# Fillings of the expert table one tile ahead, and earlier reads of the last sums, in a hybrid convolution, scan and mixture-of-experts kernel

## The chip, the cores and the metric

The kernel runs on one core of a Trainium2 chip, as a single program. The metric is the device time of one execution in microseconds (us). The engines are named as the profile names them: PE is the matrix engine and PEld its weight loads, DVE the vector engine, ACT the scalar engine, POOL is GpSimd, and SP issues most of the DMA transfers. "L2029" is line 2029 of the kernel before, unless the line is said to be of the kernel after.

## The reference

The input is x of shape (2, 256, 48, 48), float32. Two layers follow each other. Layer 0 adds to x a convolution branch and a local attention branch over 7 by 7 neighbourhoods. Layer 1 turns the picture into 2 x 2304 = 4608 tokens of 256 channels, adds a gated state-space scan, and then a mixture of 8 experts of which every token takes its best 2. The last part is what the change touches:

```python
xf = x.reshape(-1, D)                       # 4608 tokens, D = 256
gate_logits = xf @ Wg + bg                  # 8 experts
top_w, top_i = jax.lax.top_k(gate_logits, 2)
top_w = jax.nn.softmax(top_w, axis=-1)
w_dense = jnp.sum(jax.nn.one_hot(top_i, E) * top_w[..., None], axis=1)
out = jnp.zeros_like(xf)
for e in range(E):
    h = jax.nn.gelu(xf @ W1[e] + b1[e], approximate=False)   # 256 -> 1024
    out = out + w_dense[:, e:e + 1] * (h @ W2[e] + b2[e])    # 1024 -> 256
...
t = t + out.reshape(B, L, D)                # and t goes back to (2, 256, 48, 48)
```

The kernel computes only the two experts that each token takes: it sorts the tokens by expert and runs every expert over its own tokens.

## The kernel before

**The table of tokens.** While the scan of layer 1 is finished chunk by chunk, each chunk of 128 tokens is normalized, its two experts are found, and its rows (256 channels, 8 gate values and the token's number: 1060 bytes) are written by POOL's indirect transfers (L1679) into a table `xs` in DRAM. Each expert has its own part of the table, `PART` rows long, and the rows come in order of arrival. `taken` holds, for every expert, the last row that it has used.

**Tiles.** The expert stage works through the table in tiles. A pair is 256 rows of one expert, a single is 128 rows. The list `tiles` has 33 pairs with 4 singles among them. Which expert and which rows a tile has is known only when all tokens have been counted; `plan()` and `plan_tiles()` work it out on DVE from the counts, with a dozen small comparisons and sums over 33 x 8 and 8 x 8 numbers. The plan's answer is `where`, one small integer table for the pairs and one for the singles: row 0 has the first row of a tile in `xs` (L1963), row 1 the place of the expert's weights (L1964). SP loads such a number into a register when it issues a transfer. Three tiles of expert 0 have been computed earlier, beside the end of the scan (the lines up to L1843); the plan is issued behind the second to last of these (L1833 is their last step on DVE).

**Fillings.** An expert's last tile mostly runs over the end of its rows. So behind the last row of each expert a filling is written: rows of zeros (`none`) whose token numbers point to spare rows of the result. In the kernel before, `fill(e)` does that for all eight experts at the border between the scan and the expert loop (L2006, called in a loop behind the plan): 256 rows for expert 0, 128 rows for the others. Its start is `ends`, the rows of `taken` plus one, which needs no plan. The group "fill" of `declare_no_dep` tells the scheduler that a filling and the other accesses of the table in that group need not wait for each other; the group "rows" says the same for fillings and scatters.

**The loop.** For tile i, `fetch(i)` brings its rows from `xs` into `ex` (L2029, three buffers), and `load(i)` brings the biases `bt` (L2019) and the weights `wt` (L2021, 2 MB, three buffers). `turn(i)` transposes the rows on PE (L902), copies them (L904), and works out on DVE each row's gate weight (`own` L2041, `weight` L2045) and its token number (L2047). `up(i)` multiplies by the first weights (L2085) with the gelu on ACT (L2089). `weight_sums` and `hidden_sums` (L2059 to L2062, L2071 to L2074) are additions on DVE for a scheme that gets a pair's second product with 7 block products in place of 8; `down(i)` does these (L2128) and combines them (L2132 to L2141), a single goes by L2113. `finish` scales by the gate weight (L2094) and adds the rows into a table `acc` in DRAM by an indirect transfer (L2095). At the end of tile i, `fetch(i + 3)` and `load(i + 3)` are issued. All transfers of SP are kept in the order of the program; `load(i + 3)` waits for a weight buffer, that is for the last matmul of tile i.

**The end.** `results()` reads the sums from `acc` in 12 blocks of 384 tokens. The first 8 blocks are read before the last tiles are done, the last 4 ("late reads", L2201) afterwards. It goes through the blocks two by two: PE transposes them (L2226), DVE and ACT copy them (L2229), and for each pair of blocks one store goes out on SP and one on ACT (L2232). In the kernel before, the late reads are issued when the pass reaches block 8, so SP has issued its stores of blocks 0, 2, 4 and 6 ahead of them.

The scheduler orders each engine's instructions by a model of their costs; where `keep_in_program_order` is called, the order of the program holds.

Of the kernel before, what the change touches and what calls it, by code (L numbers as in the profile page):

```python
# [32 lines left out]
I32 = mybir.dt.int32  # L33
AF = mybir.ActivationFunctionType
ALU = mybir.AluOpType
AX = mybir.AxisListType

P = 128
# [27 lines left out]
TB = NJ * P  # L66
# [4 lines left out]
E, HID = 8, 1024  # L71
NHC = HID // P

TR = 256
CAP = B * N
PART = CAP + TR
EARLY, NEARLY = 3, 3
NPAIR, NSINGLE = 2 * B * N // TR - NEARLY, E
# [40 lines left out]
def bcast(ap, axis, shape):  # L119
    return ap.unsqueeze(axis).to_broadcast(shape)  # L120
# [108 lines left out]
class Kernel:  # L229
# [1625 lines left out]
    def plan(self):  # L1855

        nc, begun = self.nc, [5 * TR] * NH

        def new(*shape, dtype=F32):
            size = int(np.prod(shape))  # L1860
            h = next(h for h in range(NH) if begun[h] + size <= N)
            t = self.x[1][:, h, begun[h] : begun[h] + size]
            begun[h] += size
            if len(shape) > 1:
                names = "abc"[: len(shape)]
                t = t.rearrange(f"p ({' '.join(names)}) -> p {' '.join(names)}", **dict(zip(names[1:], shape[1:])))
            return t.bitcast(dtype) if dtype != F32 else t

        vec = nc.vector
        scratch = new(NPAIR * 2 * E)  # L1870

        def piece(*shape):
            t = scratch[:, : int(np.prod(shape))]
            names = "abc"[: len(shape)]
            return t.rearrange(f"p ({' '.join(names)}) -> p {' '.join(names)}", **dict(zip(names[1:], shape[1:])))

        last_rows = new(E, dtype=I32)
        vec.tensor_scalar(last_rows, self.taken, 1.0, None, ALU.add)
        return last_rows, partial(self.plan_tiles, new, piece)

    def plan_tiles(self, new, piece):

        nc, vec, n, k, tid = self.nc, self.nc.vector, P, CAP // TR, self.c["tid"]
        tri = self.c["tri"].rearrange("p (a b) -> p a b", a=E)
# [63 lines left out]
        for which, row, behind in ((pwhich, prow, late), (swhich, srow, None)):  # L1948
            count = which.shape[-1]
            shape = [n, count, E]  # L1950
            to, hot, past = new(2, count, dtype=I32), new(count, E), new(count)
            vec.scalar_tensor_tensor(row, which, float(PART), row, ALU.mult, ALU.add)
            vec.tensor_tensor(hot, bcast(which, 2, shape), bcast(tid[:, :E], 1, shape), ALU.is_equal)
            if behind is not None:
                own = piece(count, E)
                vec.tensor_tensor(own, hot, bcast(first, 1, shape), ALU.mult)
                vec.tensor_reduce(past, own, AX.X, ALU.add)
                vec.tensor_tensor(past, past, behind, ALU.mult)
                vec.scalar_tensor_tensor(row, past, float(TR), row, ALU.mult, ALU.add)
            vec.tensor_tensor(hot, hot, bcast(self.ahead, 1, shape), ALU.mult)  # L1960
            vec.tensor_reduce(past, hot, AX.X, ALU.add)
            vec.tensor_add(row, row, past)
            vec.tensor_scalar(to[:, 0, :], row, float(E * PART), None, ALU.min)  # L1963
            vec.tensor_scalar(to[:, 1, :], which, float(E - 1), float(P), ALU.min, ALU.mult)  # L1964
            where.append(to)
# [16 lines left out]
    def experts(self, ctx):  # L1982
# [16 lines left out]
        nfirst, load_sums = BEFORE // NJ, self.load_sums  # L1999
        tiles += [(1, i) for i in range(NUSUAL, NSINGLE)]  # L2000

        def fill(e):
            row = self.value(ends[0:1, e : e + 1], sp, NROWS - TR)
            rows = P if e else TR
            put = self.tc.keep_in_program_order(
                nc.sync.dma_start(self.expert_rows(self.xs[bass.ds(row, rows), :]), self.none[:, : rows // P])  # L2006
            )
            self.tc.declare_no_dep(put.ins, group="fill", reason="every part of the table has its own")
            self.tc.declare_no_dep(put.ins, group="rows", reason="the rows of an expert end before")
            self.tc.add_to_no_dep_group("fill", put.ins)  # L2010

        def load(i):
            halves, n = tiles[i]
# [128 lines left out]
                    finish(i, y, j)  # L2142
            del weights[i], turned[i], hidden[i]

        ends, plan_tiles = self.plan()
        with self.tc.issue_after(self.adds[NEARLY - 2].ins):
            where, many = plan_tiles()
        for e in range(E):
            fill(e)
        load(0)  # L2150
        fetch(0)
        fetch(1)
        load(1)
        load(2)
        fetch(2)
        with self.tc.issue_after(self.adds[NEARLY - 1].ins):
            turn(0)
            weight_sums(0)

        def run(first, end):  # L2160
            for i in range(first, end):
                up(i)
                if i + 1 < end:
                    turn(i + 1)
                if i in sums:
                    hidden_sums(i)
                down(i)
                if i + 1 < end:
                    weight_sums(i + 1)
                if i + 3 < end:  # L2170
                    fetch(i + 3)
                    load(i + 3)
                if i + 4 == usual:
                    for g in range(nfirst):
                        load_sums(g, "first sums")
# [2 lines left out]

        with self.tc.If(self.value(many[0:1, 0:1], list(self.nc.engines), NSINGLE) > NUSUAL):
            for i in range(usual, usual + 3):  # L2180
                fetch(i)
                load(i)
            turn(usual)
            run(usual, len(tiles))
            for g in range(nfirst):
                load_sums(g)
# [21 lines left out]
    def results(self, pool):  # L2208

        nc = self.nc  # L2210

        first, size, n = BEFORE // NJ, 2 * TB, 0
        for g in range(0, B * NBLK, 2):
            b, blk = divmod(g, NBLK)
            if g == first:
                for i in range(first, B * NBLK):
                    self.tc.keep_in_program_order(self.load_sums(i))
            for k in range(NH):
                if n % (WMAT // size) == 0:
                    space = pool.tile([P, WMAT], F32, tag="wt", name="o")  # L2220
                o = space[:, n % (WMAT // size) * size :][:, :size].rearrange("p (i t) -> p i t", i=2)
                n += 1
                for i in range(2):
                    ps = self.bank()
                    for j in range(NJ):
                        nc.tensor.transpose(  # L2226
                            ps[:, j * P : (j + 1) * P], self.sums_block(g + i)[:, j, k * P : (k + 1) * P], self.ident
                        )
                    (nc.vector.tensor_copy, nc.scalar.copy)[i](  # L2229
                        o[:, i].rearrange("c (p j) -> c j p", j=NJ), ps[:, :TB].rearrange("c (j p) -> c j p", j=NJ)  # L2230
                    )
                (nc.sync, nc.scalar)[k].dma_start(self.out[b, k * P : (k + 1) * P, blk * TB : (blk + 2) * TB], o)  # L2232

    def run(self):
        nc = self.nc
# [130 lines left out]
```

## Time and profile before

| | us |
|---|---|
| median of 3 runs | 1292.45 (1290.72 to 1294.8) |
| the profiled execution | 1295.8 |
| its span | 1294.0 |
| PE busy in the span | 1232.5 (95%), mean granted clock 0.986 |
| DVE, ACT, POOL busy | 924.8, 792.7, 557.6 |
| start of the fillings (L2006) | 753.86 |
| first fetch (L2029) | 780.83 |
| first matmul of the expert loop (L2085) | 790.70 |
| last matmul of the expert loop (L2113) | 1268.9 |
| first early store, first late read, last store issued | 1272.23, 1277.93, 1290.34 |

Times in the profile count from the start of the span. A timeline's line has the start, the length, the engine, the line, the operation, output and input; "x8" means that many instructions were put together; in brackets stands how long the engine was idle before it and what ended the wait. "issue" is a wait for nothing that the profile shows. SPq and ACTq are the queues of SP and ACT, that is the issue of their transfers, not the transfers themselves.

### The profile page before, as it was taken

What the parts mean: (1) busy time and instruction counts of PE and PEld (TensorE: products, weight loads), DVE (VectorE), ACT (ScalarE), POOL (GpSimd) and SP (SyncE); (2) the same over time, 40 slices, a digit from 0 to 9 for tenths busy, and PEclk for the clock granted to TensorE, in tenths of its full rate; (3) what the DMA queues carried; (4) which work ended last, traced back from release to release, by engine and by line L of the source; (5) the groups of instructions that cost most, each with busy time, mean ns of one, the idle gap of its engine ahead of it and who ended that gap; (6) DMA issues with size and microseconds to landing.
All of it is one profiled execution on the core that took longest, in us unless ns stands there. A gap on an engine that the chain in (4) does not pass through costs nothing. (4 is left out here: it accounts for less than half of the span.)

```text
span 1294.0 us, 23558 instructions
## 1 busy us (share of the span) xinstructions
PE 1232.5 (95%) x8048; PEld 983.4 (76%) x8048; DVE 924.8 (71%) x2425; ACT 792.7 (61%) x1954; POOL 557.6 (43%) x769
## 2 busy tenths in 40 slices
PE   4999999998799999999999997999999999999995
PEld 3566766665567777777777786999999999999994
DVE  5899999999577887879797745555654665566442
ACT  2598978898799888789697552333333333333342
POOL 4411230210357878999889963212121212221220
PEclk9999999999799999999999998999999999999998
DMA  7331322211132234333636238657667667666756
GB/s 283 126 104 41 100 92 76 80 49 41 43 107 89 91 116 120 116 114 120 187 117 186 64 133 278 184 169 254 203 221 236 192 198 228 235 188 199 233 178 208
DMA packets 101658, 194.12 MB, mean 150 GB/s; under 512 B 10635, under 2 KB 82652, under 8 KB 96604
## 3 DMA queue, kind: packets, MB, share of 16 engines
q1 hardware_dynamic: 85020, 168.51, 38.3%
q0 software_dynamic: 14400, 19.74, 7.8%
q10 hardware_dynamic: 2116, 4.33, 1.0%
q8 instruction: 66, 1.08, 0.3%
q14 instruction: 56, 0.46, 0.1%
HBM read 154.24 MB, written 43.23 MB: 153 GB/s over the span
## 5 line engine op out<-in xcount | busy, mean ns | idle before, releaser
L2095 POOL DMA_INDIRECT acc<-ey,token x70 | 108.7, 1552 | 368.5 <-ACT ey L2094 312.1
L2085 PE MATMUL bank<-ext,wt 128*128 128x256 f32 (+1 forms) x1152 | 241.3, 368 | 0.0
L2089 ACT ACTIVATE hid<-bank,bt 128x256 f32<-128x256 f32 (+1 forms) x288 | 132.3, 461 | 170.7 <-PE bank L2085 166.5
L2085 PEld LDWEIGHTS bank<-ext,wt 128*128 128x128 f32 x1152 | 207.0, 190 | 25.0
L681 POOL COPY kp<-kp 128x10 f32<-128x10 f32 (+1 forms) x60 | 24.9, 415 | 179.4 <-DVE kp L674 179.4
L592 DVE SCALAR_TENSOR_TENSOR x<-hid,w2r,x 128x1128 f32<-128x1128 f32 (+3 forms) x72 | 99.9, 1392 | 0.4 <-ACT hid L586 0.2
L2128 PE MATMUL po<-ts,ss 128*128 128x128 f32 x768 | 96.2, 275 | 0.0
L916 PE MATMUL bank<-xn,win 128*128 128x387 f32 x240 | 92.7, 510 | 2.1 <-ACT t L999 2.1
L1129 DVE SCALAR_TENSOR_TENSOR xc<-bank,vec,xc 128x384 f32<-128x384 f32 x144 | 86.6, 610 | 8.4 <-ACT xc L1118 8.1
L2128 PEld LDWEIGHTS po<-ts,ss 128*128 128x128 f32 x768 | 90.9, 192 | 0.0
L1345 ACT ACTIVATE mt<-mt,cum 128x128 f32<-128x128 f32 x288 | 87.8, 393 | 1.7 <-DMA mt<-decays 1.7
L800 ACT ACTIVATE prob<-prob,top 128x308 f32<-128x308 f32 x144 | 78.3, 552 | 16.0 <-DVE top L789 15.6
L1679 POOL DMA_INDIRECT xs<-u,rows x72 | 72.9, 1012 | 17.4 <-issue 14.7
L2132 ACT COPY u<-po 128x128 f32<-128x128 f32 x32 | 8.5, 266 | 114.2 <-PE po L2128 114.2
L2072 DVE TENSOR_TENSOR ss<-hid 128x512 f32<-128x512 f32 x32 | 22.1, 691 | 70.6 <-ACT hid L2089 70.6
L1451 PE MATMUL bank<-wout,y 128*128 128x264 f32 x288 | 72.0, 396 | 0.1
L916 PE MATMUL zbank<-xn,win 128*128 128x384 f32 x192 | 71.2, 492 | 0.5 <-ACT z L1247 0.3
L806 ACT ACTIVATE prob<-prob,rden 128x308 f32<-128x308 f32 x144 | 67.7, 550 | 3.7 <-DVE rden L855 3.7
L582 DVE SCALAR_TENSOR_TENSOR hid<-xp,vec,hid 128x1175 f32<-128x1175 f32 (+1 forms) x48 | 68.4, 1425 | 0.1
L2128 PE MATMUL po<-wt,hid 128*128 128x128 f32 x496 | 65.5, 275 | 0.0
L789 DVE CUSTOM_DVE_ANT_0 prob<-banks,cst 128x308 f32<-128x308 f32 x144 | 61.7, 471 | 3.9 <-PE banks L779 3.6
L916 PEld LDWEIGHTS bank<-xn,win 128*128 128x128 f32 x240 | 42.5, 195 | 24.8 <-issue 3.9
(334 smaller groups left out, 2989.6 us busy)
## 6 DMA issues: line engine op xcount, KB each, us to landing
wt<-in_We SPq DMA_DIRECT2D x36, 2048.0 KB
mt<-decays SPq DMA_DIRECT2D x36, 512.0 KB
ex<-xs SPq DMA_DIRECT2D x36, 265.0 KB
rd<-decays SPq DMA_DIRECT2D x68, 128.0 KB
val<-vtab SPq DMA_DIRECT2D x72, 110.0 KB
bt<-in_We SPq DMA_DIRECT2D x36, 136.0 KB
vraster<-vout SPq DMA_DIRECT2D x18, 256.0 KB
acc<-x SPq DMA_DIRECT2D x36, 128.0 KB
```

The lines of the kernel that those rows point to most:

```text
L582: nc.vector.scalar_tensor_tensor(dst, src, w[:, k : k + 1], dst, ALU.mult, ALU.add)
L592: nc.vector.scalar_tensor_tensor(dst, src, w[:, k : k + 1], dst, ALU.mult, ALU.add)
L800: nc.scalar.activation(t, t, AF.Exp, bias=T["top", c][:, a : a + 1], scale=-1.0, accum_out=T["den", c][:, a : a + 1])
L916: self.nc.tensor.matmul(ps, lhsT=lhs(k), rhs=rhs(k), start=k == 0, stop=k == NH - 1)
L1129: nc.vector.scalar_tensor_tensor(out(), T["bank", ("cv", at)][:, i : i + TB], wc[:, i : i + 1], out(), ALU.mult, ALU.add)
L1345: nc.scalar.activation(t, t, AF.Relu, bias=at_s, scale=-1.0)
L1451: nc.tensor.matmul(ps[:, : C + E], lhsT=T["y", c][:, m, :], rhs=self.l1["wout"][:, m, :], start=m == 0, stop=m == NZ - 1,)
L1679: ins = nc.gpsimd.indirect_dma_start(self.xs, bass.IndirectOffsetOnAxis(ap=of("rows")[:, i, q : q + 1], axis=0), T["u2", g][:, i, :], None,)
L2085: nc.tensor.matmul(ps[:, :rows], lhsT=w1[:, k, c * P : (c + 1) * P], rhs=xt[:, k, :], start=k == 0, stop=k == NH - 1,)
L2089: nc.scalar.activation(hid[:, c, :], ps[:, :rows], AF.Gelu, bias=bt[:, c : c + 1])
L2095: put = nc.gpsimd.indirect_dma_start(self.acc, bass.IndirectOffsetOnAxis(ap=token[:, j : j + 1], axis=0), y, None, compute_op=ALU.add)
L2128: nc.tensor.matmul(p[name], lhsT=v[a][:, c], rhs=v[w][:, c], start=c == 0, stop=c == NHC // 2 - 1)
```

## The change

The fillings are now made per tile. `where` gets a third row: for each tile, the end of its expert's rows, worked out in `plan_tiles()` by a product and a sum over the experts, with a place behind the whole table for tiles that have no expert. `fill(i)` writes 128 rows there, and is called one tile ahead of the fetch that may need them: `fill(0)` (256 rows, by `first_end`, which needs no plan) and `fill(1)` ahead of the loop, then `fill(i + 4)` behind `load(i + 3)`. The group "fill" is gone, so that the scheduler orders fillings and fetches of the table: a fetch waits until the filling before it has landed, and a filling until the fetch before it has landed. `fill(i)` is called for every tile, so an expert's filling is written again for each of its tiles. In `results()` the late reads are issued when the pass reaches block 4 in place of block 8, that is behind SP's second store; and the stores are kept in the order of the program.

```diff
@@ -1869,16 +1869,17 @@
         vec = nc.vector
         scratch = new(NPAIR * 2 * E)
 
-        def piece(*shape):
-            t = scratch[:, : int(np.prod(shape))]
+        def piece(*shape, at=0):
+            t = scratch[:, at : at + int(np.prod(shape))]
             names = "abc"[: len(shape)]
             return t.rearrange(f"p ({' '.join(names)}) -> p {' '.join(names)}", **dict(zip(names[1:], shape[1:])))
 
-        last_rows = new(E, dtype=I32)
+        last_rows, first_end = new(E), new(1, dtype=I32)
         vec.tensor_scalar(last_rows, self.taken, 1.0, None, ALU.add)
-        return last_rows, partial(self.plan_tiles, new, piece)
-
-    def plan_tiles(self, new, piece):
+        vec.tensor_copy(first_end, last_rows[:, 0:1])
+        return first_end, partial(self.plan_tiles, new, piece, last_rows)
+
+    def plan_tiles(self, new, piece, last_rows):
 
         nc, vec, n, k, tid = self.nc, self.nc.vector, P, CAP // TR, self.c["tid"]
         tri = self.c["tri"].rearrange("p (a b) -> p a b", a=E)
@@ -1948,9 +1949,15 @@
         for which, row, behind in ((pwhich, prow, late), (swhich, srow, None)):
             count = which.shape[-1]
             shape = [n, count, E]
-            to, hot, past = new(2, count, dtype=I32), new(count, E), new(count)
+            to, hot, past, end = new(3, count, dtype=I32), piece(count, E, at=NPAIR * E), new(count), new(count)
             vec.scalar_tensor_tensor(row, which, float(PART), row, ALU.mult, ALU.add)
             vec.tensor_tensor(hot, bcast(which, 2, shape), bcast(tid[:, :E], 1, shape), ALU.is_equal)
+            own = piece(count, E)
+            vec.tensor_tensor(own, hot, bcast(last_rows, 1, shape), ALU.mult)
+            vec.tensor_reduce(end, own, AX.X, ALU.add)
+            vec.tensor_scalar(past, which, float(E), float(E * PART), ALU.is_ge, ALU.mult)
+            vec.tensor_tensor(end, end, past, ALU.max)
+            vec.tensor_copy(to[:, 2, :], end)
             if behind is not None:
                 own = piece(count, E)
                 vec.tensor_tensor(own, hot, bcast(first, 1, shape), ALU.mult)
@@ -1999,15 +2006,17 @@
         nfirst, load_sums = BEFORE // NJ, self.load_sums
         tiles += [(1, i) for i in range(NUSUAL, NSINGLE)]
 
-        def fill(e):
-            row = self.value(ends[0:1, e : e + 1], sp, NROWS - TR)
-            rows = P if e else TR
+        def fill(i):
+            if i >= len(tiles):
+                return
+            halves, n = tiles[i]
+            at = where[2 - halves][0:1, 2, n : n + 1] if i else first_end[0:1]
+            row = self.value(at, sp, NROWS - TR)
+            rows = P if i else TR
             put = self.tc.keep_in_program_order(
                 nc.sync.dma_start(self.expert_rows(self.xs[bass.ds(row, rows), :]), self.none[:, : rows // P])
             )
-            self.tc.declare_no_dep(put.ins, group="fill", reason="every part of the table has its own")
             self.tc.declare_no_dep(put.ins, group="rows", reason="the rows of an expert end before")
-            self.tc.add_to_no_dep_group("fill", put.ins)
 
         def load(i):
             halves, n = tiles[i]
@@ -2142,17 +2151,19 @@
                     finish(i, y, j)
             del weights[i], turned[i], hidden[i]
 
-        ends, plan_tiles = self.plan()
+        first_end, plan_tiles = self.plan()
         with self.tc.issue_after(self.adds[NEARLY - 2].ins):
             where, many = plan_tiles()
-        for e in range(E):
-            fill(e)
+        fill(0)
         load(0)
         fetch(0)
+        fill(1)
         fetch(1)
         load(1)
         load(2)
+        fill(2)
         fetch(2)
+        fill(3)
         with self.tc.issue_after(self.adds[NEARLY - 1].ins):
             turn(0)
             weight_sums(0)
@@ -2170,6 +2181,8 @@
                 if i + 3 < end:
                     fetch(i + 3)
                     load(i + 3)
+                    if i + 4 < end:
+                        fill(i + 4)
                 if i + 4 == usual:
                     for g in range(nfirst):
                         load_sums(g, "first sums")
@@ -2178,8 +2191,10 @@
 
         with self.tc.If(self.value(many[0:1, 0:1], list(self.nc.engines), NSINGLE) > NUSUAL):
             for i in range(usual, usual + 3):
+                fill(i)
                 fetch(i)
                 load(i)
+            fill(usual + 3)
             turn(usual)
             run(usual, len(tiles))
             for g in range(nfirst):
@@ -2212,7 +2227,7 @@
         first, size, n = BEFORE // NJ, 2 * TB, 0
         for g in range(0, B * NBLK, 2):
             b, blk = divmod(g, NBLK)
-            if g == first:
+            if g == first // 2:
                 for i in range(first, B * NBLK):
                     self.tc.keep_in_program_order(self.load_sums(i))
             for k in range(NH):
@@ -2229,7 +2244,9 @@
                     (nc.vector.tensor_copy, nc.scalar.copy)[i](
                         o[:, i].rearrange("c (p j) -> c j p", j=NJ), ps[:, :TB].rearrange("c (j p) -> c j p", j=NJ)
                     )
-                (nc.sync, nc.scalar)[k].dma_start(self.out[b, k * P : (k + 1) * P, blk * TB : (blk + 2) * TB], o)
+                self.tc.keep_in_program_order((nc.sync, nc.scalar)[k].dma_start(
+                    self.out[b, k * P : (k + 1) * P, blk * TB : (blk + 2) * TB], o
+                ))
 
     def run(self):
         nc = self.nc
```

## The prediction

> **What bounds the kernel now.** I read the busy shares, then stretches of 50 us, then the queue, matmul, vector and GpSimd timelines around the two places the diff touches: the border before the expert loop (753 to 800 us) and the end (1270 us on).
>
> ```profile
> span 1294.0 us, 23558 instructions
> PE 1232.5 (95%) x8048; PEld 983.4 (76%) x8048; DVE 924.8 (71%) x2425; ACT 792.7 (61%) x1954; POOL 557.6 (43%) x769
> ```
> ```profile
> 900.00:950.00 50.00, 50.00 (x349) 47.03 (x348) 30.86 (x80) 15.88 (x37) 10.98 (x7) 1.00 0.61 189
> 950.00:1000.00 50.00, 50.00 (x337) 46.71 (x336) 27.60 (x74) 19.19 (x47) 12.39 (x8) 1.00 0.72 230
> ```
>
> The second fence has stretch, length, then busy time of PE, PEld, DVE, ACT and POOL, the granted clock, the DMA share and GB/s. From 800 to 1250 us PE is busy 50.00 of every 50.00 us: the loop is bound by matmuls, and what the change adds there costs nothing unless it makes PE wait. So time can come or go only at the border and at the end.
>
> The border, as queue, matmul, vector and GpSimd timelines (start, length, engine, line):
>
> ```profile
> 753.86 8.32 SPq L2006 DMA_DIRECT2D xs<-none  x8
> 780.83 4.00 SPq L2029 DMA_DIRECT2D ex<-xs  x2
> 785.88 0.34 SPq L2021 DMA_DIRECT2D wt<-in_We  x1
> 788.08 3.24 SPq L2029 DMA_DIRECT2D ex<-xs  x2
> ```
> ```profile
> 775.09 1.89 PE L1805 MATMUL bank<-x,wt 128*128 128x256 f32 x8
> 783.62 5.70 PE L1821 MATMUL bank<-wt,x 128*128 128x256 f32 x16 [6.64 <-issue]
> 789.15 0.60 PE L902 MATMUL bank<-cst,ex 128*128 128x128 f32 x4
> ```
> ```profile
> 783.74 0.26 DVE L1963 TENSOR_SCALAR x<-x 128x33 int32<-128x33 f32 x2 [0.16 <-DVE x L1962]
> 789.35 0.69 DVE L1833 TENSOR_TENSOR x<-bank,wt 128x512 f32<-128x512 f32 x1 [5.36 <-PE bank L1821]
> ```
> ```profile
> 763.46 0.19 POOL L1663 CAST u<-cst 128x2 int32<-128x2 f32 x1 [2.40 <-ACT u L1670]
> ```
>
> The eight fillings are long done when the last scatter lands (777.94 by its semaphore). What ends the border is PE: 6.64 us idle with nothing to wait for in sight, then 16 matmuls in 5.70 us where two groups of 8 take 2 x 1.89 = 3.78. In that stretch DVE, too, moves in steps of about 0.7 us between small operations.
>
> The loop, one tile (SP, then DVE):
>
> ```profile
> 934.23 0.33 SPq L2021 DMA_DIRECT2D wt<-in_We  x1
> 935.12 0.39 SPq L2029 DMA_DIRECT2D ex<-xs  x1
> 936.41 0.34 SPq L2019 DMA_DIRECT2D bt<-in_We  x1
> ```
> ```profile
> 943.46 0.16 DVE L2047 COPY token<-ex 128x2 int32<-128x2 int32 x1
> 944.19 0.17 DVE L2041 TENSOR_TENSOR own<-ex,bt 128x16 f32<-128x16 f32 x1
> 945.51 0.29 DVE L2133 TENSOR_TENSOR ey<-po,u 128x128 f32<-128x128 f32 x1 [1.15 <-ACT u L2132]
> ```
>
> By the semaphores these weights land at 942.18 (7.95 us after issue), `ex` at 942.84, `bt` at 943.20. The next weights follow 13.60 us after the last, so SP is idle for some 11.5 us per pair.
>
> The end:
>
> ```profile
> 1272.23 5.39 SPq L2232 DMA_DIRECT2D out<-o  x4
> 1277.93 4.07 SPq L2201 DMA_DIRECT2D x<-acc  x4
> 1287.00 2.89 SPq L2232 DMA_DIRECT2D out<-o  x2
> ```
> ```profile
> 1284.24 5.37 PE L2226 MATMUL bank<-cst,x 128*128 128x128 f32 x24 [7.44 <-DMA x<-acc]
> ```
>
> The four late reads go out behind four SP stores, and PE stands 7.44 us for them: a DMA-bound end with a hole in it.
>
> **The change, part by part.** The sum is made on the profiled execution, 1295.8 us (span 1294.0, 1.8 around it). It lies 3.35 above the median of the runs, 1292.45, and I carry the difference over unchanged.
>
> *Late reads.* The reads move from behind SP's fourth store to behind its second (1274.02 + 0.34); with 0.3 for their own addresses and the lane waits, the first is issued near 1274.65, 3.3 us earlier. Stores g=4 and g=6 of SP move behind the reads. What can be won is the hole. The twelve transfers of 384 KB up to the last read land from 1275.23 to 1287.15, one per 1.08 us; the last four stores at 1290.05, 1290.97, 1291.90 and 1292.86. Between 1287.15 and 1290.05 one transfer (about 1.0) is done in 2.90 us: 1.9 us empty. If stores g=8 are issued by 1284, there is always a transfer queued, and the last lands 1.9 earlier. A second slow stretch, 1280.20 to 1282.58 for one transfer, is 1.4 too long; it lies where the reads start beside stores, and may move or go. So -1.9 to -3.3; I take **-2.5**, the middle, as nothing tells whether the slow stretch stays. If the reads merely delay SP's two stores to the end, -1.0.
>
> [...]
>
> *Fillings, border.* Seven of eight leave SP at 754 to 762 (8.32 us of issue, in time in which SP waits 15.1 us for the scatters afterwards): 0 on the path. In their stretch POOL idles 2.40 us at 763.46, since a scatter lands in 4.5 us instead of about 2.3; that goes, and POOL's scatters and accumulates come up to 2.4 earlier. But the border's last wait is PE's, whose matmuls run without a gap until 776.98, so I take 0; the ends are -2.4 and 0.
>
> New waits: fill(1) waits for fetch(0) to land and for the plan, fetch(1) for fill(1), and behind fetch(1) SP holds the weights of tiles 1 and 2. Fillings of one size larger or equal landed in 1.9 to 2.7 us, so fetch(1) goes from 784.4 to about 786.5 and the weights about 2.3 us later, 788.2; with 8.69 us of transfer as before they land at 796.9. Tile 1's matmuls begin at 804.40: hidden by 7.5. fill(2) stands in the ring behind 4 MB of weights and lands near 802, fetch(2) near 804.5, its reader on DVE (own, L2041) runs at 807.98: hidden by 3. If the cover went, DVE would hold the sums of the next tile, one microsecond for one.
>
> *Longer plan.* Twelve operations in plan_tiles and one copy at the head. By their like: 264-wide multiply and reduce 0.43 each (L1956, L1957), 64-wide 0.22 each, nine small ones 0.17: 0.86 + 0.44 + 1.5 = 2.8, less overlap 2.6 us. DVE waits 5.36 us after the plan, so 0; without the stall of PE it would be up to +1.6 (below).
>
> *Fillings, loop.* About 36 times 132.5 KB (4.8 of 194 MB) and on SP about 1.0 us (a register load, register arithmetic, the issue of 0.33). Per tile the chain is: weights issued at 0, filling in the place that `ex` has now, landing at about 8.6; fetch issued at 8.9, landing near 11; bt issued near 10.2, landing near 12; next weights allowed at about 11 against the 13.60 at which PE frees them: 2.6 us spare. In the built order DVE's token and own for that tile have moved behind L2133 (11.3 to 11.6 us after the weights), and the operation behind them waits 1.14 us for PE anyway, with a further 2.5 us of DVE idle before the next sums: 0. After a single tile (7.46 us between weights) SP is about 3 us late and the pair behind it makes it up; weights are wanted two tiles after their issue. The ends: 0 and 0.3 us a tile, x 33 = +10.
>
> Sum: -2.5 + 0 + 0 + 0: 1293.3 profiled, **1290.0** against the median.
>
> **The rivals.** (A) is the sum: 1288.5 to 1291.5 by the ends of the reads.
>
> (B) The border's stall goes or shrinks with the fillings' traffic. For it: the steps of 0.7 us are on SP too, from 760 us, amid the fillings. Against: it lasts until 784, and the last filling landed by 764.1. Price: without the stall the plan loses its 4.5 us of steps and ends at 779.5, with the longer one 782.1; the last L1833 runs there instead of 789.35, so up to -7.2, half of it -3.6: 1283 to 1286. [...]
>
> (C) There is no stall in timed runs, and the plan is the border's bound: L1821 would end at 776.98 + 3.78 = 780.8, the plan at 782.1 : +1.3, with the later fetch(2) up to +3: 1290 to 1293.
>
> (D), the other side: fetches land too late for DVE's place. It decides when fill, fetch and bt land beyond about 12.7 us after the weights (1.1 later than estimated as the place of own) and DVE can't make it up. At 0.3 us a tile 1300.
>
> (E) The end is full anyway: only 1.0 gained, 1291.5.
>
> **How the numbers follow.** 0.3% is 3.9 us, about what a measurement of this kernel can tell from no change. A 0.42 (a third of it faster by that, as the median of before has itself a spread of 4 us), B 0.28 (faster), C 0.08, E 0.06 (same), D 0.16 (slower). Faster 0.15 + 0.28 = 0.43, same 0.27 + 0.14 = 0.41, slower 0.16. The range leaves out the lower tenth of B and the upper part of D: 1283 to 1296.
>
> **What would show it.** The reads (new line near L2216) issued at 3 to 3.5 us earlier against the end, and no 1.9 us hole before the last four stores: right. PE busy 50.00 of 50 in the loop: no D; token or own waiting on DMA for more than 1 us, with PE idle behind it: D. PE's idle time before the last L1821 tells A from B. Wrong would be a wait of the plan's readers (fill(1)) that reaches tile 1's matmuls, or a transfer that the reads push behind the last store.

## The result and the profile after

The kernel after takes 1311.14 us (median of 4 runs, 1303.73 to 1316.97) against 1293.46 for the kernel before (1290.72 to 1294.8): a ratio of 1.0133, 95% interval 1.0101 to 1.0165. It is some 17 us slower, where the forecast was 2.5 us faster; it lies above the range. The profiled execution of the kernel after took 1303.73 us, the shortest of its four, so its trace shows less than half of the usual loss (7.9 us of span).

Lines of the kernel after are up to 15 higher than those of the kernel before: the fetch is L2038, the filling L2017, `bt` L2028, `wt` L2030, own L2050, token L2056, the first matmuls L2094, the gelu L2098, the scaling L2103, the end's reads, transposes and stores L2216, L2241, L2247.

The page, and two stretches of 50 us (stretch, length, busy time of PE, PEld, DVE, ACT and POOL, granted clock, DMA share, GB/s):

```profile
span 1301.9 us, 23691 instructions
PE 1232.6 (95%) x8048; PEld 981.4 (75%) x8048; DVE 928.8 (71%) x2436; ACT 790.8 (61%) x1954; POOL 556.8 (43%) x769
```
```profile
900.00:950.00 50.00, 47.90 (x322) 44.40 (x321) 28.07 (x70) 16.61 (x39) 11.30 (x7) 1.00 0.76 231
950.00:1000.00 50.00, 50.00 (x354) 47.19 (x353) 31.04 (x81) 18.06 (x44) 10.84 (x7) 1.00 0.70 213
```

PE is busy for the same time in all (1232.6 against 1232.5 us), so the loss stands in this trace as idle time of PE. And the loop is no longer full: between 900 and 950 us 2.1 us are missing. The place, as timelines of SP, DVE, ACT and PE:

```profile
912.63 0.33 SPq L2030 DMA_DIRECT2D wt<-in_We  x1
913.95 0.35 SPq L2017 DMA_DIRECT2D xs<-none  x1
924.09 0.38 SPq L2038 DMA_DIRECT2D ex<-xs  x1
925.11 0.34 SPq L2028 DMA_DIRECT2D bt<-in_We  x1
```
```profile
922.06 0.29 DVE L2142 TENSOR_TENSOR ey<-po,u 128x128 f32<-128x128 f32 x1 [1.24 <-ACT u L2141]
926.70 0.17 DVE L2056 COPY token<-ex 128x2 int32<-128x2 int32 x1 [4.35 <-DMA ex<-xs]
927.64 0.17 DVE L2050 TENSOR_TENSOR own<-ex,bt 128x16 f32<-128x16 f32 x1 [0.77 <-DMA bt<-in_We]
930.73 0.75 DVE L2150 TENSOR_TENSOR ey<-ey,bt 128x256 f32<-128x256 f32 x2
```
```profile
926.98 0.47 ACT L2098 ACTIVATE hid<-bank,bt 128x256 f32<-128x256 f32 x1 [0.39 <-PE bank L2094]
931.17 0.91 ACT L2103 ACTIVATE ey<-ey,weight 128x256 f32<-128x256 f32 x2 [3.73 <-DVE ey L2150]
931.99 2.15 ACT L2098 ACTIVATE hid<-bank,bt 128x256 f32<-128x256 f32 x5
```
```profile
932.49 1.13 PE L2094 MATMUL bank<-ext,wt 128*128 128x256 f32 x4 [2.10 <-ACT hid L2098]
```

Read from top to bottom this is a chain of five links. The filling stands behind 2 MB of weights in SP's queue and lands at 924.07 by its semaphore, 10.12 us after its issue. The fetch can be issued only then. DVE waits 4.35 us at `token` and 0.77 at `own` for that fetch and for `bt`. The sums of the tile that is being finished (`ey`, L2142 to L2150) are queued behind these two, so ACT's scaling L2103 waits 3.73. Behind the scaling ACT has the gelus of the next tile, and PE, whose next matmuls wait for a bank that the gelu L2098 releases, stands 2.10 us. The rows that DVE waits for are needed only two tiles later: PE transposes them at 947.06. The whole loop has three such stops of PE, of 2.10, 1.92 and 0.42 us, 4.4 of the 5.5 us that it lost; for the rest matmuls took longer.

The border:

```profile
775.90 0.71 SPq L2038 DMA_DIRECT2D ex<-xs  x1
783.62 0.37 SPq L2017 DMA_DIRECT2D xs<-none  x1
785.69 0.38 SPq L2038 DMA_DIRECT2D ex<-xs  x1
787.11 0.35 SPq L2030 DMA_DIRECT2D wt<-in_We  x1
```
```profile
765.94 3.72 PE L1805 MATMUL bank<-x,wt 128*128 128x256 f32 x16 [2.08 <-issue]
780.14 3.78 PE L1821 MATMUL bank<-wt,x 128*128 128x256 f32 x8 [10.48 <-ACT x L1813]
792.90 0.60 PE L902 MATMUL bank<-cst,ex 128*128 128x128 f32 x4
```
```profile
758.85 0.19 POOL L1663 CAST u<-cst 128x2 int32<-128x2 f32 x1 [0.56 <-ACT u L1670]
```

POOL's pause of 2.40 us is down to 0.56, and fetch(0) goes out 4.9 us earlier. PE's stall is still there, comes some 7 us earlier, when more of the early tiles' matmuls are still to be done, and is longer (2.08 and 10.48 us in place of 6.64). The first matmul of the loop is at 794.44, 3.74 later than before. The end:

```profile
1281.47 2.14 SPq L2247 DMA_DIRECT2D out<-o  x2
1283.91 3.81 SPq L2216 DMA_DIRECT2D x<-acc  x4
1287.82 9.22 SPq L2247 DMA_DIRECT2D out<-o  x4
```
```profile
1289.37 0.94 PE L2241 MATMUL bank<-cst,x 128*128 128x128 f32 x6 [3.32 <-DMA x<-acc]
1291.97 1.51 PE L2241 MATMUL bank<-cst,x 128*128 128x128 f32 x6 [1.66 <-DMA x<-acc]
```

The reads go out 2.4 us behind the first store, not 5.7, and PE's wait of 7.44 is now 3.32, 1.66 and 0.25. From the first transpose to the end of the span it takes 22.10 us in place of 23.41.

So the trace divides into three stages. *Border* is the time from the first matmul of the early tiles (L1805) to the first matmul of the loop, *loop* from there to the end of its last matmul, *end* from the first transpose of the results to the end of the span; all are worked out from the starts and ends of matmuls in the traces. The runs told of below are in it, too.

| kernel | border | loop | end | span |
|---|---|---|---|---|
| before | 63.0 | 478.2 | 23.4 | 1294.0 |
| after | 69.5 | 483.7 | 22.1 | 1301.9 |
| e1 reads only | 64.9 | 478.2 | 22.4 | 1297.3 |
| e2 fills only | 68.3 | 498.2 | 23.4 | 1317.2 |
| e3 fill ahead | 66.4 | 478.4 | 22.1 | 1293.0 |
| e4 spare traffic | 63.0 | 478.2 | 23.9 | 1293.7 |
| e5 late gate | 66.1 | 478.2 | 22.0 | 1292.8 |
| e6 plan only | 60.8 | 478.2 | 22.6 | 1288.7 |
| e7 ahead, late gate | 61.6 | 478.2 | 21.7 | 1286.8 |
| e9 reads, late gate | 63.3 | 478.2 | 21.8 | 1294.5 |
| f1 after again | 69.4 | 486.0 | 22.2 | 1308.0 |
| f2 fill twice | 69.3 | 524.3 | 21.8 | 1344.4 |
| f3 reads first | 63.3 | 478.2 | 22.1 | 1291.1 |
| f4 reads again | 62.1 | 478.2 | 22.0 | 1288.5 |
| g1 spare border | 61.6 | 484.2 | 21.9 | 1293.7 |
| g2 fills behind | 62.3 | 478.2 | 25.3 | 1292.6 |
| g3 late gate again | 68.9 | 478.2 | 21.9 | 1297.2 |

What is left of a span is the time ahead of the first L1805, which lies between 723.6 and 730.0 us without any order, and 1.7 us between loop and end.

### The profile page after: what moved, and what is told of

It is laid out like the page before. It is cut to its first block, busy times and chain, and to the rows that moved or that the text cites. A ratio compares the mean times of both kernels' runs of the same rounds, so it can differ in the third digit from the quotient of the medians.

```text
span 1301.9 us, 23691 instructions
## 1 busy us (share of the span) xinstructions
PE 1232.6 (95%) x8048; PEld 981.4 (75%) x8048; DVE 928.8 (71%) x2436; ACT 790.8 (61%) x1954; POOL 556.8 (43%) x769
## 5 line engine op out<-in xcount | busy, mean ns | idle before, releaser
L2094 PE MATMUL bank<-ext,wt 128*128 128x256 f32 (+1 forms) x1152 | 242.3, 368 | 4.4 <-ACT hid L2098 4.4
L2098 ACT ACTIVATE hid<-bank,bt 128x256 f32<-128x256 f32 (+1 forms) x288 | 130.2, 459 | 165.2 <-PE bank L2094 153.8
L2094 PEld LDWEIGHTS bank<-ext,wt 128*128 128x128 f32 x1152 | 206.7, 190 | 30.8 <-ACT hid L2098 6.0
L2081 DVE TENSOR_TENSOR ss<-hid 128x512 f32<-128x512 f32 x32 | 22.1, 691 | 56.3 <-ACT hid L2098 56.3
## 6 DMA issues: line engine op xcount, KB each, us to landing
xs<-none SPq DMA_DIRECT2D x36, 132.5 KB
```

Source lines behind the costliest of these rows:

```text
L2094: nc.tensor.matmul(ps[:, :rows], lhsT=w1[:, k, c * P : (c + 1) * P], rhs=xt[:, k, :], start=k == 0, stop=k == NH - 1,)
L2098: nc.scalar.activation(hid[:, c, :], ps[:, :rows], AF.Gelu, bias=bt[:, c : c + 1])
```

## The experiments

**Theories.** Theory 1: the chain of fetch, filling and weights on SP makes fetches late, and DVE, ACT and PE wait for them in turn. Theory 2: the traffic of the new fillings slows the weights. Theory 3: the late reads hurt the end. They were run apart first.

**e1, the reads alone.** The kernel before with

```diff
-            if g == first:
+            if g == first // 2:
```

and the stores in program order.

> The late reads alone: the kernel before with the four late reads behind SP's second store and the stores in program order; the fillings stay at the border. If the loss comes from the fillings (theory 1, the chain fetch - filling - weights on SP; theory 2, the fillings' traffic), this kernel shows none of it: the loop keeps PE at 50.00 of 50, and the end (first L2226 matmul to the end of the span) is 1.4 us shorter, as between the two profiles shown (23.4 us before, 22.0 after): about 1292 against 1293.5. If the reads are the loss (theory 3), the time is 1300 or more.

Measured: 1293.06 against 1294.17, ratio 0.9987 (0.9974 to 1.0001). The loop is untouched and the end 1.0 us shorter in its profile, which fell on the longest of its eleven runs. Theory 3 falls.

**e2, the fillings alone.** The kernel after with the end of the kernel before.

> The fillings alone: the kernel after with the reads and stores of the end as in the kernel before. Theories 1 and 2: slower than before by about as much as the whole change, +10 to +20 us (1303 to 1313), with idle PE in the loop. Theory 3: as before, 1293 within 3 us.

Measured: 1303.13, ratio 1.0067 (1.0049 to 1.0084), five runs from 1300.56 to 1319.22. That is the lower edge of what was expected. The profile fell on the longest of these runs and shows how far the loop can go. Waits of DVE and of PE in the loop, 815 to 1255 us (total, times, longest):

```profile
DVE token L2056 <- DMA ex<-xs: 41.8, 19, 6.2
DVE own L2050 <- DMA bt<-in_We: 30.7, 26, 4.6
```
```profile
PE bank L2094 <- ACT hid L2098: 7.8, 3, 2.7
PE po L2137 <- DVE ss L2080: 1.6, 2, 0.8
PE bank L2094 <- ACT ey L2103: 1.6, 1, 1.6
```

In the kernel before the first two lines are 4.4 and 1.8 us in all. Of the 19.9 us that this loop is longer, PE is idle for 13.1. The rest is matmuls that took longer, 5.1 us of it by reckoning in three stretches of 3.41 us in which the granted clock was 0.50, each beside a stop of PE of 2.1 to 2.7 us. The ratio lies below that of the whole change (1.0133) although the end is not shortened; between five executions the loss differs by 19 us, and why it was smaller in four of them is open.

**e4, the traffic without the waits.** The kernel before with a write of 128 rows into a table `spare` behind each tile's weights:

```diff
                     fetch(i + 3)
                     load(i + 3)
+                    if i + 4 < end:
+                        spend(i + 4)      # 128 rows of `none` into `spare`, as fill() does into `xs`
```

> The kernel before with the traffic of the new fillings added and none of their waits: behind each tile's weights SP writes 128 rows into a spare table that nobody reads; the eight fillings at the border stay. Theory 2 (traffic): as slow as the change, 1303 to 1313. Theory 1 (chain): no fetch waits for these writes, so within 3 us of before, 1291 to 1297.

Measured: 1294.63, ratio 1.0006 (0.9997 to 1.0016), loop 478.23 us. The same bytes at the same place of SP's queue cost nothing as long as no fetch waits for them. Theory 2 falls.

**e3, the filling ahead of the weights.** The kernel after with

```diff
                     fetch(i + 3)
-                    load(i + 3)
                     if i + 4 < end:
                         fill(i + 4)
+                    load(i + 3)
...
         fetch(1)
+        fill(2)
         load(1)
         load(2)
-        fill(2)
```

> The kernel after with one line moved: each filling is issued ahead of the weights of the tile before it, not behind them, so that it never stands behind 2 MB in SP's queue; the number of fillings, their bytes, the longer plan and the late reads are those of the kernel after. Theory 1 (the chain): the loop's loss of some 5.5 us in the profile goes, PE is busy 50.00 of 50 again, and the time falls to about 1293 to 1297 (what the border costs, 3.7 us in the profile shown, may stay). Theory 2 (the traffic): it stays at 1303 to 1313.

Measured: 1297.26, just above the expected range, ratio 1.0027 (1.0016 to 1.0038), loop 478.43 us. Most of the loss is gone. DVE still waits for fetches, less and in other places:

```profile
DVE own L2050 <- DMA bt<-in_We: 15.8, 15, 2.6
DVE token L2056 <- DMA ex<-xs: 11.2, 10, 1.8
```

The filling now lands 2.1 us after its issue (median, 7.9 in the kernel after) but waits for a fetch that lands 7.9 us after its own, so the chain is about as long: after the first single tile the weights go out 10.7, 11.1, 12.9 and 13.8 us apart (10.6, 12.3, 13.4 and 14.3 in the kernel after). What is shorter is DVE's wait, as the fetch lands 8.8 us after the weights' issue in place of 11.9 (medians).

**e5, the readers one tile later.** The kernel after with DVE's three small operations on a fetched tile issued behind the copy of that tile's transposes:

```diff
-            self.transposes(
+            copy = self.transposes(
                 xt.rearrange("p k q -> p (k q)"),
...
+            with self.tc.issue_after(copy.ins):
+                gate(i, halves, x, bt, xt)      # own, weight and token, as before
```

> The kernel after with DVE's three small reads of a fetched tile (own, weight, token) issued behind the copy of that tile's transposes, one tile later than the scheduler had put them, so that DVE no longer stands in front of a fetch that has just been issued; fillings, SP's order and the chain of fetch, filling and weights are those of the kernel after. If PE's idle time in the loop comes by way of DVE's wait (theory 1 in full: SP's chain, then DVE's wait, then ACT's scaling in front of the gelus, then PE), the loop goes back to 478 to 479 us and the time to 1293 to 1298. If SP's chain itself starves PE (late weights), or the traffic does, the loop stays at 484 us or more and the time above 1302.

Measured: 1294.98, ratio 1.0018 (1.0002 to 1.0034), loop 478.23 us. Its stretches are full again:

```profile
900.00:950.00 50.00, 50.00 (x350) 47.02 (x349) 30.29 (x80) 15.81 (x38) 9.32 (x6) 1.00 0.75 228
950.00:1000.00 50.00, 50.00 (x337) 46.73 (x336) 27.06 (x72) 19.32 (x47) 13.13 (x9) 1.00 0.75 226
```

This is the decisive run. SP's chain is as it was: fetches still wait for fillings behind the weights, and the weights land 8.7 us after their issue (median; 8.4 in the kernel after, 8.0 before). DVE has not one wait for a fetch left in the loop, and PE none at all. So it is not that weights or rows come too late for PE; it is the place at which DVE asks for them.

**e7, both remedies.**

> Both remedies in the kernel after: fillings issued ahead of the weights, and own, weight and token one tile later. If what was left of the loss with the fillings ahead (1297.3 against 1294.2, although the end is 1.3 shorter) was still DVE's wait on a fetch, this comes to 1292.5 to 1294.5. If it lies at the border or in the plan, it stays near 1297.

Measured: 1295.29, ratio 1.0011 (0.9993 to 1.003), loop 478.23 us. It is no better than e5, within what the intervals tell: what e3 had left of the loss lies mostly outside the loop (478.43 us in its own profile, the shortest of its runs).

**e9, what the later place costs by itself.** The kernel of e1 with the edit of e5.

> The kernel before with the late reads behind SP's second store and own, weight and token one tile later; the eight fillings stay at the border. It tells what the later place of these three costs or gives by itself: by theory 1 nothing, since DVE waits for no fetch in the kernel before, so as with the reads alone, 1293 within 1.5 us.

Measured: 1294.19, ratio 1.0006 (0.9991 to 1.002): nothing that the runs can tell.

**e6, the longer plan alone.** The kernel before with the added operations of `plan()` and `plan_tiles()`, whose third row nobody reads.

> The kernel before with the longer plan alone: the thirteen added DVE operations are made, and nobody reads their answer. If the plan's 2.6 us stand on the border's path: +1 to +3, 1295 to 1297. If DVE's wait behind the plan covers them: within 1 us of before, 1293 to 1295.

Measured: 1294.59, ratio 1.001 (0.9995 to 1.0024). The border of its profile is the shortest of all (60.8 us). At most a part of the loss, and perhaps none. (The added operations are eleven, not the thirteen of the expectation: DVE counts 2425 before, 2436 here and in the kernel after.)

**f1, the change again.** On another chip, with a second profile.

> The kernel after, unchanged, beside the kernel before on another chip and with a second profile. Theory 1: the loop is longer than 478.2 us by the waits of DVE for fetches, by an amount that differs between executions (5.5 and 19.9 us in the two profiles so far of this place of the fillings), the end is 22.1 us, the border again anything from 785 to 795; slower than before by 8 to 18 us. If the first measurement was a matter of that chip: within 4 us of before.

Measured: 1312.4, ratio 1.0138 (1.0115 to 1.0161). The loss of its profile, 14.0 us against the trace of before: 1.0 ahead of the border, 6.4 in the border, 7.75 in the loop, -1.2 at the end.

**f2, one link more.** The kernel after with every filling from the second on written twice:

```diff
-            put = self.tc.keep_in_program_order(
+            for _ in range(2 if i else 1):
+                put = self.tc.keep_in_program_order(
```

> The kernel after with every filling from the second on written twice, one after the other: the suspected chain gets one more link of 2 to 2.5 us per tile, and the traffic grows by 4.8 MB, which cost nothing without waits. Theory 1: the chain per pair goes from 11 to 13 us to 13.5 to 15.5, past the 13.60 us that PE needs, so the weights are issued late in most tiles, DVE waits in most tiles, and the time rises far over that of the kernel after: 1325 to 1370. If the chain were not the cause, the time would stay at that of the kernel after.

Measured: 1349.11, ratio 1.0435 (1.0404 to 1.0466), loop 524.3 us. One link more per tile costs 37 us more than f1 in the same measurement. Of the 46 us that its loop is longer, PE is idle for 31; the rest is longer matmuls, and three stretches of the loop (3.41, 6.83 and 6.83 us) have a granted clock of 0.50. The weights are now issued 13.7 to 16.2 us apart in most tiles, and are themselves late (waits of DVE and PE in the loop, 815 to 1255 us, lines of this kernel):

```profile
DVE token L2057 <- DMA ex<-xs: 55.8, 17, 9.6
DVE own L2051 <- DMA bt<-in_We: 46.5, 24, 4.0
DVE ts L2069 <- DMA wt<-in_We: 35.1, 14, 3.5
```
```profile
PE bank L2095 <- ACT hid L2099: 14.2, 3, 5.0
PE bank L2095 <- DMA wt<-in_We: 8.0, 10, 1.3
```

The lines with `wt` are new: here the chain has become longer than PE's 13.60 us per pair. In the kernel after it had not; there only DVE's place was hurt.

**f3 and f4, the reads.** The reads behind SP's first store (`first // 4`), and e1 again.

> The kernel before with the late reads behind SP's first store in place of the second. If the end is bound by 16 transfers of about 1 us that follow one another without a hole, as the profile with the reads behind the second store shows, nothing more is to be won: the end at 22.0 to 22.8 us and the time as with the reads behind the second store, 1291 to 1294. If reads that come sooner still shorten it: another 0.5 to 1.5 us. A wait of SP for the last accumulates, with its later stores behind it, would make it longer than 23.

> The reads alone once more (behind SP's second store, fillings at the border), with more rounds, to settle whether they beat the kernel before: by the end's 1.0 us in the first profile 0.9992, by the first measurement 0.9987.

Measured: 1292.81, ratio 0.9985 (0.9971 to 0.9998), and 1292.08, ratio 0.9987 (0.9974 to 1.0001). The two results of e1 and f4, the same kernel, carry the same ratio and interval; by the medians it was 1.1 us faster than before in the one and 3.1 in the other. The end is 22.1 and 22.0 us. Reads that come sooner still win nothing more. The twelve kernels with early reads end in 21.7 to 22.4 us, those with the reads of before in 22.6 to 25.3. These two are the fastest versions that were found; their lead of 0.13 to 0.15% over the kernel before is at the edge of what the runs can tell.

**g1, the border's traffic put back.** What the loop left unexplained is the border: 68.3 to 69.5 us in four profiles with the fillings of the kernel after (66.1 in e5, which has them too), 60.8 to 64.9 in the seven with eight fillings at the border. The kernel after with seven writes into a spare table where the seven fillings were:

```diff
         fill(0)
+        spare = nc.dram_tensor("spare", (E * PART, XW), F32).ap()
+        for e in range(1, E):
+            self.value(first_end[0:1], sp, NROWS - TR)
+            self.tc.keep_in_program_order(
+                nc.sync.dma_start(self.expert_rows(spare[e * PART : e * PART + P, :]), self.none[:, :1])
+            )
         load(0)
```

> The kernel after with seven writes of 128 rows into a spare table at the place of the seven fillings that the change took from the border; nobody waits for their data. If the border is longer in the kernel after because that traffic is gone (POOL's scatters without their pause), the stretch from the first L1805 to the first matmul of the loop goes back to 61 to 65 us, and the time falls by about 6, to 1304 to 1308. If the new waits or the plan lengthen it, it stays at 68 to 70 us and the time at 1309 to 1314. The loop loses 5 to 20 us as before.

Measured: 1304.77, ratio 1.0102 (1.0052 to 1.0152), four runs from 1296.12 to 1310.45; border 61.6 us, loop 484.2. The median is 6 to 8 us below those of the kernel after, as expected if work that nobody needs makes it faster. But the intervals of the ratios overlap (1.0101 to 1.0165 and 1.0115 to 1.0161 for the kernel after), and the profile fell on the shortest of the four runs. POOL and PE at its border:

```profile
761.62 0.19 POOL L1663 CAST u<-cst 128x2 int32<-128x2 f32 x1 [3.98 <-ACT u L1670]
```
```profile
772.43 1.89 PE L1805 MATMUL bank<-x,wt 128*128 128x256 f32 x8
778.24 6.31 PE L1821 MATMUL bank<-wt,x 128*128 128x256 f32 x16 [3.92 <-ACT x L1813]
784.38 0.60 PE L902 MATMUL bank<-cst,ex 128*128 128x128 f32 x4
```

POOL's pause is back (3.98 us), and PE's stall is again a single one behind the last L1805.

**g2, the border's traffic taken away.** The kernel before with the fillings of experts 1 to 7 issued behind the fetch of tile 0.

> The kernel before with the seven fillings issued behind the fetch of tile 0, so that their traffic no longer lies between the scatters; plan, loop and end are those of the kernel before. If the missing traffic lengthens the border: 66 to 70 us for that stretch, +3 to +6, 1297 to 1301. If not: 61 to 65 us and within 2 us of before.

Measured: 1297.0, ratio 1.0033 (1.0014 to 1.0053): slower by 3.5 us, as expected of the missing traffic, though the seven fillings now also stand ahead of fetch(1) and of the weights of tiles 1 and 2 in SP's queue. Its profile, the second shortest of ten runs, does not show it where it was expected: border 62.3 us, end 25.3, and the weights of tile 1 still in time (landed at 797.81, first matmul at 801.07). So time and trace don't agree here, and the place stays open in this run.

**g3, the late gate again.**

> The kernel after with the three small DVE reads one tile later, again, for a second profile: loop 478.2 us again (theory 1), end 22 us, and the border's stretch at 66 (as in its first profile), if a border of its own size is what leaves it 1.5 us behind the kernel before; at 61 to 65 if its first profile was the scatter of executions.

Measured: 1295.99, ratio 1.0013 (0.9993 to 1.0033), border 68.9, loop 478.23 us. The loop is whole for the second time. The border differs by 2.8 us between two profiles of one kernel.

Taken together: without the seven fillings between the scatters the border is 61.6 to 69.5 us (nine profiles, mean 66.9), with that traffic 60.8 to 64.9 (eight, mean 62.8). g1 and the time of g2 point to the traffic's absence as the cause; it is not shown, since e7 and g2, without that traffic, have 61.6 and 62.3 us, and by what mechanism it would act is not settled.

The times give a second account of how the loss divides. The later place of DVE's three operations alone takes the ratio from 1.0133 and 1.0138 to 1.0018 and 1.0013, which is some 15 of the 17 us, though these are measurements on different chips. The loops of the two traces of the kernel after account for 5.5 and 7.75 of them; both fell on the shortest of their four runs, and e2's loop shows that 20 can be lost there, but where the rest lay in the executions without a trace stays open. What remains with the later place, with the reads' gain of 0.13% added back, leaves some 4 us for the border, the longer plan included.

## Why the prediction was wrong, point by point

**The loop, put at 0: the step that failed.** Counted from the issue of the weights, the filling landed at 8.8 us in the median, near the 8.6 estimated, but up to 11.4; the fetch at 11.9 and up to 14.0, not near 11; `bt` at 13.0 and up to 15.6, not near 12. Where nothing else held it, the chain needed 10 to 13 us from weights to weights, not about 11. So the step "SP is about 3 us late and the pair behind it makes it up" was wrong: after the first single tile the weights were issued 10.6, 12.3, 13.4 and 14.3 us apart (after the others much the same), and DVE met a late fetch for three or four tiles. That the operations behind own and token wait 1.14 us for PE anyway, and DVE has 2.5 more, was taken as cover for them. The wait reached 5.1 us; and the cover counted only what DVE has next, not that ACT's scaling stands in front of the gelus. The working did ask who waits for DVE, but only as far as the next sums. The loop's loss was 5.5, 7.75 and 19.9 us in the traces of the kernel after, f1 and e2.

**Rival D** was this mechanism, with the right place (DVE behind a late fetch), the right point of decision (beyond about 12.7 us after the weights: in the tile shown `bt` landed 14.98 us after, and even the median was 13.0), the sign that was named for it (token or own waiting for a DMA with PE idle behind) and a price of 10 us that lies among the measured 5.5 to 20. It was given 0.16 because the durations of one tile of the kernel before were used for a chain whose lateness adds up.

**The border, put at 0 with ends of -2.4 and 0.** It was +6.5 and +6.4 us in the two profiles of the kernel after, and by the times some 4, the longer plan included. The working looked only for a gain in traffic that goes; rival B, that the stall shrinks with the fillings, had the sign the wrong way round. The stall grew, and in the profile of g1 it was back to a single one of 3.92 us.

**The new waits at the border** (fill(1), fetch(1), fill(2)) were hidden, as said: fetch(1) went out at 785.69 against an estimate of 786.5, tile 1's first matmul came 13.70 us after tile 0's, as in the kernel before (804.40 - 790.70). The 8.69 us of transfer that the working takes for tile 1's weights do not come out of the trace of before, where they landed at 795.65, 9.77 us after their issue; they took 7.72 in the kernel after, so nothing came of it.

**The longer plan, put at 0 with an end of +1.6.** e6: +1.3 us, with an interval from -0.6 to +3.1 (0.9995 to 1.0024 of 1293.5): not told apart from 0. DVE still had 6.61 us to wait behind it. The working counts two operations too many (thirteen for eleven), so by its own lengths the plan is 2.5 us longer before overlap, not 2.8; that, too, was covered.

**The reads, put at -2.5 (-1.9 to -3.3).** The mechanism was right and the size was too large by the traces: -1.3 in that of the kernel after. The medians of e1, f3 and f4 differ from before by -1.1 to -3.1, which does not settle it. The hole ahead of the last four stores is closed, as argued (1.9 us). But the slow stretch did not go: where the reads start beside the stores the rate falls to 200 to 225 GB/s for 1.2 us in the trace of after, too, and 0.6 of the hole was lost again among the transfers. Where, is open. The hole alone, 1.9 us, the lower end of the estimate, was nearer than its middle.

**The other rivals.** A wants no idle PE in the loop and falls with it; by the reads' ends of -3.3 and -1.0 it reaches from 1289.2 to 1291.5, not from 1288.5. C (no stall in timed runs, and the plan as the border's bound) is not shown: DVE had 5.36 us to wait behind the plan before the change, 6.61 after it, 1.29 in e7. E (only 1.0 gained at the end) was nearly the size of it.

## What to carry to other kernels

Before a transfer is made to wait for another, ask where that other one stands in its queue: here a write of 132.5 KB cost nothing behind 2 MB of weights, and what waited for it had to wait some 8 us, up to 10. Then follow each wait through every engine that has other work queued behind it, past the first cover, to the engine that bounds the kernel: here the wait was for rows that were needed two tiles later, and moving their three small readers was enough to make it harmless. And where tiles have two lengths, look at the short one: here a chain of 10 to 13 us fitted the pairs (13.60 us of PE) and not a single (7.46 us), and the debt was paid over the next three or four tiles.

## What the runs showed of the hardware

PE's stall at the border is in all 17 profiles: 3.9 to 10.5 us of idle time in the early tiles, counting the longest piece, in all but one (2.8 in e7). The granted clock of 0.80 to 0.95 over 760 to 795 us (0.90 in the kernel before, 0.85 in the kernel after), against 1.00 in the loop of the kernel after, is a mean of stretches of 1.00 and of 0.50. In every one of the 17 traces one or two stretches of 0.50 lie there, 3.41 to 13.66 us together, at or behind the idle time: from 780.83 to 787.66 in the kernel before, from 774.58 to 784.82 in the kernel after. Matmuls ran slower in them: 8 of L1821 took 3.78 us in the kernel after, where 8 had taken 1.89. That fits the 16 matmuls in 5.70 us that the working had noted; so the 8 cost 1.89 us beside the idle time ahead of them.

The stall's length differs between executions of the same instructions (7.58 us in e1, 5.26 in f4). The spans of e1 and f4 differ by 8.8 us, 5.4 of it ahead of the border and 2.8 in it; those of e5 and g3 by 4.4, 1.6 and 2.8. With the traffic of seven writes of 132.5 KB ahead of it, the longer stops of PE in the early tiles added up to 3.9 to 7.6 us (eight profiles), without it to 4.9 to 12.6 (nine). What the stall is, and whether it is there when nothing is recorded, no run here shows.

The weights landed a median of 8.0 us after their issue where fetches stood behind them, and 8.4 to 8.8 where fetch and `bt` went out just ahead (kernel after, e2, f1). Why was not tried.
